# A perceiver layer with a mixture of experts: 64-row context tails, a routine for up to 96 left-over tokens of an expert, and a group split into halves

## The chip, the cores and the metric

The kernel runs on one core of a Trainium2 chip, in fp32. The metric is the device time of one execution, in microseconds. Three runs of the kernel before took 663.93, 663.94 and 664.02 us, so the median is 663.94 us.

## What is computed

There are 8 batches of 64 latent rows (x, width 512) and a context of 1601 rows of width 512 for each batch. Three residual blocks follow each other, each on a layer-normalized x:

```
x = x + relu( softmax( p (ctx W^T + b)^T ) ctx W^T + b )          p = layernorm(x)
x = x + attention block: causal linear attention (16 heads of 64, features elu(q proj) + 1),
        then a gelu MLP of width 2048, each on a layernorm with gain and shift
x = x + mixture of experts: 8 experts, each token sent to its best two, weights = softmax of the two logits,
        expert(x) = (silu(x w0) * (x w1)) wo        hidden width 1024
```

The first block's softmax runs over all 1601 context rows of a batch. The router picks two of eight experts for each of the 512 tokens, so there are 1024 pairs of token and expert, and how many fall to each expert is known only while the kernel runs.

## The kernel before

**Attention to the context.** The 512 latent rows stand in four tiles (NT = 4) of 128 rows; a tile holds two batches, 64 rows of each. `key_group(t, g)` multiplies the tile with a quarter of its two batches' transposed context (401 or 398 keys) into scores; when the fourth quarter is there, `softmax(t)` follows. `turn_scores(t)` transposes the exponentials back (three banks of 512 keys and one of what is left), and `weigh(t, g)` multiplies them with 512 context rows at a time, for both batches. 1601 rows are 3 x 512 and a tail of 65, which is loaded as a tile of 65 partitions, two batches beside each other (line 188), and multiplied at line 487. The result is scaled by 1 / sum on VectorE (line 495), transposed (`turn_av`) and multiplied with W (`attended`). The loop over t writes this order out by hand: between `weigh` steps of tile t stand the key groups of tiles t + 1 and t + 2, and for the last two tiles the value products (`values`, line 537) of the next block.

**The stream of loads.** Nearly all big inputs are loads of about 1 MB issued by SyncE (SP) in one list, `order`, built ahead of time; `issue_to` (lines 177 to 195) gives them out in that order as buffers of a ring of 12 come free. Each issue takes the next of eight semaphores and waits until the load that had it before has landed, so about eight loads are under way. For tile t the list has rows 0, keys 2 of the next tile, rows 1, keys 3, rows 2, the tail, then keys 0 and 1 of tile t + 2. Some small loads don't belong to the list: `late_loads` (lines 407 to 412: zeroes for a spare part of the output and for a table, b2 to all partitions, and the small projection twice) is issued when the loop reaches t = 1, after `weigh(1, 2)`, and so is `centre_router` (lines 544 to 557: eight TensorE instructions with 8 columns, and one on VectorE).

**The attention block and the MLP** run from about 172 to 405 us on TensorE without a gap that matters, and the change doesn't touch them.

**The experts.** For each expert e the first 128 of its tokens are one whole tile; the rows are gathered by an indirect DMA on GpSimd (`fetch`, line 1136) and transposed (`turn_tile`, line 1154). `whole_tile` multiplies them with four quarters of the up weights (line 1200; a quarter is 256 columns of w0 and 256 of w1), gates them on ScalarE and VectorE (lines 1163 and 1165), transposes the hidden values (line 1171) and accumulates the output (line 1208). `add_rows` scales the output by the gate on ScalarE (line 1180) and adds it to the result in memory by an indirect DMA (line 1181); these additions follow each other.

What an expert has beyond 128 tokens is found from `count` at run time. With 129 to 160 tokens `few` is 1 and `group(e)` runs right behind the whole tile: up to 32 rows, with the four quarters of the weights in four column groups of the array at once (line 1238), one gate, two transposes, line 1249 for the four partial outputs, and a product with `fold` (line 1259) that adds the four. With more than 160, all the rest goes to whole tiles of their own at the end of the program (`big_tile`, `all_big`), which load that expert's weights once more. The branches are at line 1429 (a group) and line 1433 (a big tile). All engines take them: each has read the counts into registers (`load_few`, `load_big`). An engine that skips a body waits for its own earlier work and raises its semaphores by what the body would have.

PSUM has two sets of banks here: `side_bank(0)` and `y_bank(0)` for whole tiles, `side_bank(1)` (two banks) and `y_bank(1)` (one) for groups, and one bank for transposed tokens.

Of the kernel before, what the change touches and what calls it, by code (L numbers as in the profile page):

```python
# [15 lines left out]
F32 = mybir.dt.float32  # L16
AF = mybir.ActivationFunctionType
ALU = mybir.AluOpType
# [9 lines left out]
TAIL = LK - NG * GK  # L28
# [7 lines left out]
R = P // NQ  # L36
NI = B * S // P
# [9 lines left out]
def perceiver_kernel(  # L47
# [127 lines left out]
    def issue_to(n):  # L175

        while issued[0] < min(n, len(order)):
# [8 lines left out]
            elif key[0] == "tail":  # L186
                t_ = tails.tile([P, 2, D], F32, tag="tail", name="_".join(str(k) for k in key))
                nc.sync.dma_start(t_[:TAIL, :, :], src)
# [261 lines left out]
    def turn_scores(t):  # L450
# [5 lines left out]
        for g in range(NG + 1):  # L456
# [6 lines left out]
            else:  # L463
                nc.tensor.transpose(bank[:TAIL, :P], scores[:, NG * GK : LK], ident)
                nc.scalar.copy(e_t[:TAIL, 4 * NG, :], bank[:TAIL, :P])

    all_av, all_xo = {}, {}

    def weigh(t, g):
# [15 lines left out]
        if g == NG - 1:  # L485
            for h in range(2):
                nc.tensor.matmul(
                    av[h * S : (h + 1) * S, :],
                    e_t[:TAIL, 4 * NG, h * S : (h + 1) * S],
                    need("tail", t)[:TAIL, h, :],  # L490
                    start=False,
                    stop=True,
                )
            av_sb = all_av[t] = xa2.tile([P, D], F32, tag="tmp", name=f"av_sb_{t}")
            nc.vector.tensor_scalar(av_sb, av, all_rinv[t], None, ALU.mult)
# [66 lines left out]
    for t in range(NT):  # L562
# [15 lines left out]
        if t == NT - 3:  # L578
            late_loads()
            centre_router()  # L580
# [530 lines left out]
    if True:  # L1111
# [36 lines left out]
        def turn_tile(key, n=P):  # L1148
# [8 lines left out]
            xg_t = moe2.tile([P, KC, n], F32, tag=f"xgT{n}", name=f"xgT_{key[0]}_{key[1]}")  # L1157
# [18 lines left out]
        def add_rows(key, y, n, side):  # L1176
# [3 lines left out]
            nc.scalar.activation(y_sb[:n, :], y[:n, :], AF.Copy, scale=gate[:n, :])  # L1180
# [10 lines left out]
        def whole_tile(key, up_of, down_of, between=lambda k: None):  # L1191
# [5 lines left out]
            def up(q):  # L1197
                bank = side_bank(0, f"up_{nm}_{q}")
# [4 lines left out]
                return gated(0, bank, f"{nm}_{q}")  # L1203
# [10 lines left out]
            h_t0 = hidden_t(0, hid0, f"{nm}_0")  # L1214
            hid2 = up(2)
            y = y_bank(0, f"y_{nm}")
            down(0, h_t0)
            h_t1 = hidden_t(0, hid1, f"{nm}_1")
            between(0)
            hid3 = up(3)  # L1220
            h_t2 = hidden_t(0, hid2, f"{nm}_2")
            down(1, h_t1)
            between(1)
            h_t3 = hidden_t(0, hid3, f"{nm}_3")
# [3 lines left out]
            add_rows(key, y, P, 0)  # L1228

        def group(e, up_of, down_of):  # L1230
# [4 lines left out]
            bank = side_bank(1, f"up_{nm}")  # L1235
            for c in range(KC):
                for q in range(NQ):
                    nc.tensor.matmul(  # L1238
                        bank[q * R : (q + 1) * R, :],
                        xg_t[c],  # L1240
                        up_of[q][:, c, :],
                        start=(c == 0),
                        stop=(c == KC - 1),
                    )
            h_t = hidden_t(1, gated(1, bank, nm), nm)
            bank = side_bank(1, f"yq_{nm}")
            for j in range(2):
                for q in range(NQ):
                    nc.tensor.matmul(
                        bank[q * R : (q + 1) * R, :],  # L1250
                        h_t[:, j, q * R : (q + 1) * R],
                        down_of[q // 2][:, 2 * (q % 2) + j, :],
# [3 lines left out]
            parts = moe2.tile([P, D], F32, tag="parts", bufs=1, name=f"parts_{nm}")  # L1256
            evacuate(parts, bank)
            y = y_bank(1, f"y_{nm}")
            nc.tensor.matmul(y[:R, :], fold, parts, start=True, stop=True)
            add_rows((e, 1), y, R, 1)  # L1260

        if True:
# [8 lines left out]

            few = moe.tile([P, NE], F32, name="few")
            more = moe.tile([P, NE, NI - 1], F32, name="more")
            nc.vector.tensor_scalar(more[:, :, 0], count, float(P + R), None, ALU.is_gt)
            nc.vector.scalar_tensor_tensor(few, count, float(P), more[:, :, 0], ALU.is_gt, ALU.subtract)
# [4 lines left out]
            def load_few():  # L1280
                _, values = nc.values_load_multi_w_load_instructions(
                    few_i, min_val=0, max_val=1, skip_runtime_bounds_check_because=counted
# [5 lines left out]
            control = moe.tile([1, 1 + 2 * NBIG], mybir.dt.int32, name="control")  # L1288
# [242 lines left out]
```

## Time and profile before

| what | value |
|---|---|
| median of three runs | 663.94 us |
| the profiled execution's own time | 665.04 us |
| its span, first to last instruction | 663.3 us |
| mean granted TensorE clock | 0.987 |
| TensorE waiting for context rows (line 477) | 6.3 us, 4 times |
| first up product of the experts starts | 417.26 us |
| groups that ran | experts 0, 3 and 5 |
| whole tiles at the end | 1 |
| last matmul ends | 651.98 us |
| e_up loads, 1 MB each | 32 and 4 for the whole tile at the end |

The profile is one execution. A row of a timeline has the start in us, the length, the engine, the line of the code, the operation with its output and inputs, the shape and a count; in brackets stands how long the engine had been idle and what ended that. TensorE does an fp32 product in two instructions, so "x32" is 16 products. A row of stretches has its bounds, its length, the busy time of PE (TensorE), PEld (its weight loads), DVE (VectorE), ACT (ScalarE) and POOL (GpSimd), each with its number of instructions, then the granted clock as a share of full speed, the busy share of the 16 DMA engines, and GB/s. A name with a q, such as POOLq, is that engine's sequencer. In the 40 slices of the page one slice is 16.6 us, and a digit is a share in tenths.

### The profile page before, as it was taken

The numbers are of one execution on the slowest core, as the hardware profiler recorded it, in microseconds if no ns is written. First come the engines' busy times: TensorE is split into PE (matmuls) and PEld (weight loads), VectorE is DVE, ScalarE is ACT, GpSimd is POOL, SyncE is SP. The second block draws the span as 40 slices with busy tenths as digits, with TensorE's granted clock in tenths as the row PEclk, the third lists the DMA queues.
The fourth block names the chain that finished last, engine by engine and source line by source line (L and its number), as shares of the span: only waits on it lengthen the run. The fifth ranks groups of instructions, "written<-read, shape, count | busy, mean of one in ns | idle before, by whom it ended". The sixth has DMA issues, their size and how long they took to land. (4 is left out here: it accounts for less than half of the span.)

```text
span 663.3 us, 6862 instructions
## 1 busy us (share of the span) xinstructions
PE 624.8 (94%) x2688; PEld 292.5 (44%) x2688; DVE 175.4 (26%) x421; ACT 128.9 (19%) x242; POOL 61.8 (9%) x82
## 2 busy tenths in 40 slices
PE   4998999899999999999999999999999899999993
PEld 3743434243444444455444458434444344344441
DVE  4011323123315878760000045311211011100100
ACT  2241222220132222031101211211111111111110
POOL 2000000000000000050000012240201202200000
PEclk9998999899999999999999999999999999999997
DMA  8999999999430303030311313139379567594611
GB/s 325 418 424 398 423 393 422 381 394 417 178 126 3 126 1 127 1 126 1 126 64 63 116 74 133 64 96 365 139 280 377 178 279 246 202 385 155 263 16 19
DMA packets 24224, 138.08 MB, mean 208 GB/s; under 512 B 4164, under 2 KB 4164, under 8 KB 11896
## 3 DMA queue, kind: packets, MB, share of 16 engines
q1 hardware_dynamic: 20056, 129.90, 49.8%
q0 software_dynamic: 3024, 6.58, 4.4%
q10 hardware_dynamic: 1104, 1.07, 0.5%
q8 instruction: 25, 0.41, 0.3%
q14 instruction: 15, 0.12, 0.0%
HBM read 132.56 MB, written 4.97 MB: 207 GB/s over the span
## 5 line engine op out<-in xcount | busy, mean ns | idle before, releaser
L1200 PE MATMUL up<-e_up,xgT 128*128 128x512 f32 x224 | 100.2, 595 | 1.2 <-PEq L1429 1.2
L1200 PEld LDWEIGHTS up<-e_up,xgT 128*128 128x128 f32 x224 | 40.9, 190 | 50.4 <-issue 50.4
L1208 PE MATMUL y<-e_wo,hidT 128*128 128x512 f32 x128 | 61.0, 599 | 0.0
L477 PE MATMUL av<-ctx,eT 128*64 128x512 f32 x192 | 51.3, 648 | 6.3 <-DMA ctx<-in_ctx_dram 6.3
L1165 DVE TENSOR_TENSOR mid<-up,act 128x256 f32<-128x256 f32 x35 | 14.8, 425 | 159.4 <-ACT act L1163 159.4
L809 PE MATMUL hid<-v_sb,w 128*128 128x512 f32 (+2 forms) x144 | 56.6, 545 | 0.0
L830 PE MATMUL mlp<-w,hid_sb 128*128 128x512 f32 x112 | 51.0, 597 | 0.0
L428 PE MATMUL sc<-ctxT,pw_t 128*64 128x401 f32 (+1 forms) x256 | 46.6, 501 | 0.0
L809 PEld LDWEIGHTS hid<-v_sb,w 128*128 128x128 f32 x144 | 26.2, 190 | 29.1 <-issue 27.3
L1163 ACT ACTIVATE act<-up 128x256 f32<-128x256 f32 x35 | 13.3, 384 | 103.7 <-PE up L1200 94.9
L1181 POOL DMA_INDIRECT out_dram<-y_sb,dst_late x11 | 16.8, 1530 | 159.9 <-ACTq L1429 103.7
L824 POOL TENSOR_TENSOR xin<-xin,b_bc 128x512 f32<-128x512 f32 x4 | 5.1, 1265 | 283.2 <-DVE rstd_h L766 279.0
L830 PEld LDWEIGHTS mlp<-w,hid_sb 128*128 128x128 f32 x112 | 20.7, 190 | 23.5 <-issue 23.4
L1208 PEld LDWEIGHTS y<-e_wo,hidT 128*128 128x128 f32 x128 | 22.4, 190 | 19.5 <-issue 19.1
L428 PEld LDWEIGHTS sc<-ctxT,pw_t 128*64 128x64 f32 x256 | 20.6, 136 | 23.4 <-issue 21.7
L477 PEld LDWEIGHTS av<-ctx,eT 128*64 128x64 f32 x192 | 14.7, 146 | 36.1 <-issue 27.5
L728 PE MATMUL wo<-wo,a_t 128*128 128x512 f32 x64 | 29.1, 600 | 0.6 <-DVE a_t L704 0.6
L617 PE MATMUL wk<-h_t,wk 128*128 128x512 f32 x64 | 29.5, 603 | 0.0
L617 PE MATMUL wq<-h_t,wq 128*128 128x512 f32 x64 | 29.4, 602 | 0.0
L537 PE MATMUL v<-wv,h_t 128*128 128x512 f32 x64 | 28.7, 597 | 0.6 <-DVE h_t L524 0.6
L702 DVE RECIPROCAL rden<-rden 128x512 f32<-128x512 f32 x8 | 26.8, 3353 | 0.3
L878 DVE TENSOR_TENSOR xs<-mlp,xs 128x512 f32<-128x512 f32 x3 | 2.1, 692 | 86.6 <-PE mlp L830 86.6
(245 smaller groups left out, 642.6 us busy)
## 6 DMA issues: line engine op xcount, KB each, us to landing
e_up<-in_L_ffn_up_dram SPq DMA_DIRECT2D x32, 1024.0 KB, 7.7
ctx<-in_ctx_dram SPq DMA_DIRECT2D x24, 1024.0 KB, 17.1
ctxT<-in_ctx_T_dram SPq DMA_DIRECT2D x24, 802.0 KB, 15.7
e_wo<-in_L_ffn_wo_dram SPq DMA_DIRECT2D x16, 1024.0 KB, 10.6
w<-in_L_attn_w_dram SPq DMA_DIRECT2D x8, 1024.0 KB, 9.8
ctxT<-in_ctx_T_dram SPq DMA_DIRECT2D x8, 796.0 KB, 16.4
big_up<-in_L_ffn_up_dram SPq DMA_DIRECT2D x4, 1024.0 KB, 7.7
wv<-in_L_attn_wv_dram SPq DMA_DIRECT2D x2, 1024.0 KB, 13.0
```

The lines of the kernel that those rows point to most:

```text
L428: nc.tensor.matmul(sc[h * S : (h + 1) * S, :width], pw_t[:, c, (2 * t + h) * S : (2 * t + h + 1) * S], keys[h][:, c, :], start=(c == 0), s ...
L477: nc.tensor.matmul(av[h * S : (h + 1) * S, :], e_t[:, 4 * g + j, h * S : (h + 1) * S], rows[h][:, j, :], start=(g == 0 and j == 0), stop=F ...
L537: nc.tensor.matmul(bank, h_t[:, c, t * P : (t + 1) * P], wv_n[:, c, :], start=(c == 0), stop=(c == KC - 1))
L617: nc.tensor.matmul(bank, w[:, c, (j % 4) * P : (j % 4 + 1) * P], h_t[:, c, :], start=(c == 0), stop=(c == KC - 1),)
L702: nc.vector.reciprocal(rden, rden)
L728: nc.tensor.matmul(wo_banks[t], a_t[:, j, t * P : (t + 1) * P], wo_r[j // 4][:, j % 4, :], start=(j == 0), stop=(j == nj - 1),)
L809: nc.tensor.matmul(hid_banks[f][:, tokens], w[:, c, (f % 4) * P : (f % 4 + 1) * P], h2_t[:, c, tokens], start=(c == 0), stop=(c == KC - 1),)
L830: nc.tensor.matmul(acc[t], hid[:, t * P : (t + 1) * P], need("w2", f // 4)[:, f % 4, :], start=(f == 0), stop=(f == FF // P - 1),)
L1165: nc.vector.tensor_tensor(hid, bank[:, FQ:], act, ALU.mult)
L1181: nc.gpsimd.indirect_dma_start(out=out, out_offset=bass.IndirectOffsetOnAxis(ap=dst[:n, :], axis=0), in_=y_sb[:n, :], in_offset=None, boun ...
L1200: nc.tensor.matmul(bank, xg_t[c], up_of[q][:, c, :], start=(c == 0), stop=(c == KC - 1))
L1208: nc.tensor.matmul(y, h_t[:, j, :], w[:, 2 * (q % 2) + j, :], start=(q + j == 0), stop=(q + j == NQ))
```

## The change

- **Level tails.** TAIL is 64; the tail tile holds all 128 partitions, 64 rows of one batch above 64 of the other, and beside them the last context row of each batch, repeated on its 64 partitions. Two products of 64 x 64 take the place of the transpose of 65 keys, the tail's products take 64 rows each, and the last row is added on VectorE by a multiply-add, after which the scaling by 1 / sum is an operation of its own.
- **Late loads and the router's centring** run at t = 2 in place of t = 1.
- **Three groups.** `few` is 2 for 129 to 160 tokens, 1 for 161 to 224 (REST = 96 left over) and 0 otherwise; only more than 224 goes to whole tiles. `three_groups` does up to 96 rows in three groups of 32, their steps interleaved. Gathers of left-over tokens take 96 rows for 32, and the scaling of the three groups' output is on VectorE.
- **The group** is split: each half of its hidden width has its own gate, and the first half is transposed between the second half's products. Outputs are made in halves of 256 columns.
- **Branches.** Both kinds of groups stand in one outer branch. What experts 6 and 7 have beyond 128 tokens and the big tiles stand in one branch ahead of expert 7's whole tile; `any` is set when any of it is there. Big tiles use group banks and expert 6's weight buffers. Instructions with a hint about a later branch are put into the whole tile's first `between`.
- Smaller: expert 7's left-over tokens are transposed during expert 6; three more small VectorE operations find `few`, three more find `any`, and one more register is loaded on each engine.

The core of the diff:

```diff
-TAIL = LK - NG * GK
+TAIL = LK - NG * GK - 1
...
+REST = 3 * R
...
-                nc.sync.dma_start(t_[:TAIL, :, :], src)
+                nc.sync.dma_start(t_, src)
...
-                nc.tensor.transpose(bank[:TAIL, :P], scores[:, NG * GK : LK], ident)
-                nc.scalar.copy(e_t[:TAIL, 4 * NG, :], bank[:TAIL, :P])
+                for h in range(2):
+                    part = slice(h * S, (h + 1) * S)
+                    nc.tensor.matmul(
+                        bank[part, :S],
+                        scores[part, NG * GK : NG * GK + TAIL],
+                        ident[part, part],
+                        start=True,
+                        stop=True,
+                    )
+                nc.scalar.copy(e_t[:, 4 * NG, :S], bank[:, :S])
...
-                    e_t[:TAIL, 4 * NG, h * S : (h + 1) * S],
-                    need("tail", t)[:TAIL, h, :],
+                    e_t[h * S : (h + 1) * S, 4 * NG, :S],
+                    need("tail", t)[h * S : (h + 1) * S, 0, :],
...
             av_sb = all_av[t] = xa2.tile([P, D], F32, tag="tmp", name=f"av_sb_{t}")
-            nc.vector.tensor_scalar(av_sb, av, all_rinv[t], None, ALU.mult)
+            nc.vector.scalar_tensor_tensor(
+                av_sb, need("tail", t)[:, 1, :], all_scores[t][:, LK - 1 : LK], av, ALU.mult, ALU.add
+            )
+            nc.vector.tensor_scalar(av_sb, av_sb, all_rinv[t], None, ALU.mult)
...
         weigh(t, 2)
-        if t == NT - 3:
+        if t == NT - 2:
...
         def group(e, up_of, down_of):
...
+            split = "p (w n) -> p w n"
+            halves = [slice(h * P, (h + 1) * P) for h in range(2)]
+            hid, h_t = [], {}
+
+            def turn(j):
+                bank = side_bank(1, f"ht_{nm}_1") if j else y_bank(1, f"ht_{nm}_0")
+                nc.tensor.transpose(bank[:, :P], hid[j], ident)
+                h_t[j] = moe2.tile([P, P], F32, tag="hidT1", name=f"hidT_{nm}_{j}")
+                (nc.scalar.copy if j else nc.vector.tensor_copy)(h_t[j], bank[:, :P])
+
+            for h in range(2):
+                bank = side_bank(1, f"up_{nm}_{h}")
+                for c in range(KC):
+
+                    if h == 1 and c == KC - 1:
+                        turn(0)
+                    for q in range(NQ):
+                        nc.tensor.matmul(
+                            bank[q * R : (q + 1) * R, : 2 * P].rearrange(split, w=2),
+                            xg_t[c],
+                            up_of[q][:, c, :].rearrange(split, w=2)[:, :, halves[h]],
+                            start=(c == 0),
+                            stop=(c == KC - 1),
+                        )
+                act = moe2.tile([P, P], F32, tag="act1", name=f"act_{nm}_{h}")
+                nc.scalar.activation(act, bank[:, :P], AF.Silu)
+                hid.append(moe2.tile([P, P], F32, tag="mid1", name=f"mid_{nm}_{h}"))
+                nc.vector.tensor_tensor(hid[h], bank[:, P : 2 * P], act, ALU.mult)
+            sums = {}
+
+            def down(j, n):
+                if j == 0:
+                    sums[n] = y_bank(1, f"yq_{nm}_1") if n else side_bank(1, f"yq_{nm}_0")
...
+                        sums[n][q * R : (q + 1) * R, : D // 2],
+                        h_t[j][:, q * R : (q + 1) * R],
+                        down_of[q // 2][:, 2 * (q % 2) + j, n * D // 2 : (n + 1) * D // 2],
                         start=(j == 0),
                         stop=(j == 1),
                     )
...
+            down(0, 0)
+            turn(1)
+            down(0, 1)
+            parts = []
+            for n in range(2):
+                down(1, n)
+                parts.append(moe2.tile([P, D // 2], F32, tag="parts", name=f"parts_{nm}_{n}"))
+                (nc.scalar.copy if n else nc.vector.tensor_copy)(parts[n], sums[n][:, : D // 2])
+            y = side_bank(1, f"y_{nm}")
+            for n in range(2):
+                nc.tensor.matmul(
+                    y[:R, n * D // 2 : (n + 1) * D // 2], fold, parts[n], start=True, stop=True
+                )
             add_rows((e, 1), y, R, 1)
+
+        def three_groups(e, up_of, down_of):
+
+            nm = f"{e}_1"
+            xg = fetched[e, 1]
...
+            hid, h_t, sums, parts = {}, {}, {}, {}
+
+            def up(g):
+                bank = side_bank(1, f"up_{nm}_{g}")
+                for c in range(KC):
+                    tokens = turned[e, 1][c] if g == 0 else xg_t3[:, c, g * R : (g + 1) * R]
+                    for q in range(NQ):
+                        nc.tensor.matmul(
+                            bank[q * R : (q + 1) * R, :],
+                            tokens,
+                            up_of[q][:, c, :],
+                            start=(c == 0),
+                            stop=(c == KC - 1),
+                        )
+                hid[g] = gated(1, bank, f"{nm}_{g}")
+
+            def turn(g):
+                bank = y_bank(1, f"ht_{nm}_{g}")
+                for j in range(2):
+                    nc.tensor.transpose(bank[:, j * P : (j + 1) * P], hid[g][:, j * P : (j + 1) * P], ident)
+                h_t[g] = moe2.tile([P, 2, P], F32, tag="hidT3", name=f"hidT_{nm}_{g}")
+                nc.vector.tensor_copy(h_t[g].rearrange("p j q -> p (j q)"), bank[:, : 2 * P])
+
+            def down(g):
+                bank = side_bank(1, f"yq_{nm}_{g}")
+                for j in range(2):
+                    for q in range(NQ):
+                        nc.tensor.matmul(
+                            bank[q * R : (q + 1) * R, :],
+                            h_t[g][:, j, q * R : (q + 1) * R],
+                            down_of[q // 2][:, 2 * (q % 2) + j, :],
+                            start=(j == 0),
+                            stop=(j == 1),
+                        )
+                parts[g] = moe2.tile([P, D], F32, tag="parts3", name=f"parts_{nm}_{g}")
+                if g < 2:
+                    nc.scalar.copy(parts[g], bank)
+                else:
+                    nc.vector.tensor_copy(parts[g][:, : D // 2], bank[:, : D // 2])
+                    nc.scalar.copy(parts[g][:, D // 2 :], bank[:, D // 2 :])
+
+            def folded(g):
+                for n in range(2):
+                    cols = slice(n * D // 2, (n + 1) * D // 2)
+                    nc.tensor.matmul(
+                        y[g * R : (g + 1) * R, cols], fold, parts[g][:, cols], start=True, stop=True
+                    )
+
+            up(0)
+            up(1)
+            turn(0)
+            up(2)
+            turn(1)
+            down(0)
+            down(1)
+            turn(2)
+            y = side_bank(1, f"y3_{nm}")
+            folded(0)
+            down(2)
+            folded(1)
+            folded(2)
+            add_rows((e, 1), y, REST, 1, by_vector=True)
...
-            nc.vector.tensor_scalar(more[:, :, 0], count, float(P + R), None, ALU.is_gt)
-            nc.vector.scalar_tensor_tensor(few, count, float(P), more[:, :, 0], ALU.is_gt, ALU.subtract)
+            nc.vector.tensor_scalar(more[:, :, 0], count, float(P + REST), None, ALU.is_gt)
+            nc.vector.tensor_scalar(few, count, float(P), 2.0, ALU.is_gt, ALU.mult)
+            over = moe.tile([P, NE], F32, name="over_few")
+            nc.vector.tensor_scalar(over, count, float(P + R), None, ALU.is_gt)
+            nc.vector.tensor_tensor(few, few, over, ALU.subtract)
+            nc.vector.tensor_tensor(few, few, more[:, :, 0], ALU.subtract)
...
+            def few_tokens(e, up_of, down_of):
+                with tc.If(few_of[e] > 0, label=f"few_{e}"):
+                    with tc.If(few_of[e] == 1, label=f"three_{e}"):
+                        three_groups(e, up_of, down_of)
+                    with tc.If(few_of[e] == 2):
+                        group(e, up_of, down_of)
+
+            def hint_ahead(e):
+
+                labels = ["last_branches"] if e == NE - 2 else [f"few_{e}", f"three_{e}"]
+                with tc.block():
+                    for label in labels:
+                        tc.mark_branch_hint_location(label, "LikelyTaken", engines=every)
...
-                    if k == 2:
+                    if k == 2 and e < NE - 1:
                         turn_tile((e, 1), R)
+                    if k == 2 and e == NE - 2:
+                        turn_tile((NE - 1, 1), R)
...
                 down_of = [need("e_wo", e, n) for n in range(2)]
+                if e == NE - 1:
+
+                    with tc.If(listed["any"] > 0, label="last_branches"):
+                        few_tokens(e - 1, *last_weights)
+                        few_tokens(e, up_of, down_of)
+                        all_big(0)
+                if e == NE - 2:
+                    last_weights.extend((up_of, down_of))
                 whole_tile((e, 0), up_of, down_of, between)
...
-                        fetch((e + 2, i), R if i else P)
+                        fetch((e + 2, i), REST if i else P)
...
-                with tc.If(few_of[e] > 0):
-                    group(e, up_of, down_of)
-
-            def all_big(j):
-                with tc.If(listed["big"] > j):
-                    big_tile(j)
-                    if j + 1 < NBIG:
-                        all_big(j + 1)
-
-            all_big(0)
```

In `weigh` the tail's products and in `issue_to` the tail's load follow from the new layout, which the host prepares. In `three_groups` the hidden values go through `gated`, as before.

## The prediction

> **What bounds the kernel now.** I read the page first, then TensorE's timeline around the attention and the experts, then the stretches of 2 us, then the records of the branches and of the end.
>
> ```profile
> PE 624.8 (94%) x2688; PEld 292.5 (44%) x2688; DVE 175.4 (26%) x421; ACT 128.9 (19%) x242; POOL 61.8 (9%) x82
> PEclk9998999899999999999999999999999999999997
> GB/s 325 418 424 398 423 393 422 381 394 417 178 126 3 126 1 127 1 126 1 126 64 63 116 74 133 64 96 365 139 280 377 178 279 246 202 385 155 263 16 19
> ```
>
> TensorE is the bound by its share, but two things differ by stage: in the first ten slices the DMA moves about 420 GB/s without a pause, and PEclk dips twice. The attention to the context is where both meet (TensorE's timeline):
>
> ```profile
> 60.99 4.91 PE L477 MATMUL av<-ctx,eT 128*64 128x512 f32 x13 [2.14 <-DMA ctx<-in_ctx_dram]
> ...
> 93.36 3.22 PE L477 MATMUL av<-ctx,eT 128*64 128x512 f32 x13 [1.00 <-DMA ctx<-in_ctx_dram]
> ...
> 127.73 6.16 PE L477 MATMUL av<-ctx,eT 128*64 128x512 f32 x13 [2.66 <-DMA ctx<-in_ctx_dram]
> ...
> 135.11 3.70 PE L537 MATMUL v<-wv,h_t 128*128 128x512 f32 x8
> ```
>
> The same 13 matmuls take 3.22 us after a wait of 1.00 us, but 4.91 and 6.16 after waits of 2.14 and 2.66. After 135 us nothing waits for the context any more. The stretches say why:
>
> ```profile
> 122.00:124.00 2.00, 1.51 (x10) 0.43 (x7) 0.00 (x0) 0.41 (x1) 0.00 (x0) 1.00 1.01 422
> 124.00:126.00 2.00, 1.04 (x2) 0.19 (x2) 1.79 (x1) 1.46 (x2) 0.00 (x0) 1.00 1.09 254
> 126.00:128.00 2.00, 0.27 (x2) 0.27 (x4) 0.03 (x1) 1.72 (x2) 0.00 (x0) 0.71 0.97 287
> 128.00:130.00 2.00, 2.00 (x6) 0.50 (x6) 0.00 (x0) 0.00 (x0) 0.00 (x0) 0.50 1.01 408
> ```
>
> The last columns are clock, DMA share and GB/s: busy engines, but only 254 and 287 GB/s. The same dip stands at 58-62 (275, 381), 90-94 (266, 354) and 146-150 us (254, 274), each where the 4 KB packets of a "tail" load of 65 rows are under way. Then the clock is half.
>
> The experts, at one group (TensorE's timeline):
>
> ```profile
> 441.05 3.64 PE L1238 MATMUL up<-e_up,xgT 128*32 128x512 f32 x32
> 445.68 0.44 PE L1171 MATMUL ht<-ident,mid 128*128 128x128 f32 x2 [0.99 <-DVE mid L1165]
> 446.73 1.92 PE L1249 MATMUL yq<-e_wo,hidT 128*32 128x512 f32 x16 [0.61 <-DVE hidT L304]
> 449.35 1.04 PE L1259 MATMUL y<-parts,fold 128*32 128x512 f32 x2 [0.70 <-ACT parts L306]
> 450.32 7.13 PE L1200 MATMUL up<-e_up,xgT 128*128 128x512 f32 x16
> ```
>
> A group costs 450.32 - 441.05 = 9.27 us, 2.3 of it stalls; three run (experts 0, 3, 5). The whole tile at the end:
>
> ```profile
> 628.90 0.65 PE L1154 MATMUL xgt_big<-ident,xg_big 128*128 128x128 f32 x4 [0.32 <-PEq L1429]
> ...
> 648.38 3.60 PE L1208 MATMUL y_big<-big_wo,hidT_big 128*128 128x512 f32 x8
> ```
>
> From 628.58 (its predecessor's end) to 651.98 it holds TensorE for 23.4 us. The inputs, put through the reference, give 133, 104, 217, 159, 87, 132, 70, 122 tokens per expert: the three groups fit, and the whole tile is expert 2's other 89.
>
> **A. Level tails, late loads (attention).** A tail DMA grows from 65 to 128 rows of 4 KB, by 0.258 MB, 0.6 us at 420 GB/s. Against it goes its dip: for the second, (420-266+420-354) x 2 us = 0.44 MB, 1.0 us; for the third (166+133) x 2 = 0.60 MB, 1.4 us; for the first (145+39) x 2, 0.9 us. The rows here that don't divide by 16 are the only ones with a dip; the Trainium skill (DMA: Bandwidth & Descriptors, "Why a DMA increments its semaphore by 16 and not by 1") has the number of DMA engines as the largest divisor up to 16, 13 for 65 rows and 16 for 128. I take the dip as gone; if it stays, nothing is gained by it. The late loads (0.58 MB, 1.4 us) stood on SP's queue at 104.9 to 113.6 us, just ahead of the context rows waited for at 127.73. They move behind the last rows, the fourth tail, wv, wq and wk. Behind them then waits wo, first used at 261 us, 100 us of cover; b2, proj and the zeroes are used later than 180 us.
>
> The rows waited for land earlier by 0.3 (first tail: 0.9-0.6), 0.4 (second), 1.4 (third, behind them) and 1.4 (late loads): 3.5 us, at 124.2. Counting 2.5 us per 1 MB load and 2.0 per key load on from the first dip, each wait in between is then 1.0 us or less, so the clock holds: 13 matmuls at 3.22 for 6.16, and the tail's at full speed, 2.9 us. The Trainium skill (TensorE: Matmul & The Clock Gate, "What's actually happening") has the clock fall after an idle window of about 3.4 us; by that rule neither wait would have cost anything and only 3.5 us would come. The rows show the fall after 2.14, so I take 2.9 more. The router's centring (L548, 8 instructions, 1.06 us) ran at 97.8 inside time that the next wait swallowed; at t = 2 it is on the path: +1.06. The tail's scores cost two matmul pairs for one transpose (0.27 us row), +0.1 to 0.2 a tile, free but for the last. VectorE's extra op (0.75 us, row of av_sb) fits: av_sb was ready 1.9 us before turn_av began. Sum -3.5 - 2.9 + 1.1 + 0.2 = **-5.1**. At best -6.9 (landing at 123.2, which the count from the first dip gives, and the tail's matmuls closer). If the dip and the half clock stay, late loads -1.4 against two longer tails +1.2 and +1.1 leave +0.9.
>
> **B. Three groups for expert 2's tile.** Up: 3 x 3.6 (L1238); hidden transposes 3 x 0.22; down 3 x 1.8 (L1249); four transposes of 96 rows 0.43; fold, twelve passes of 256 columns at 0.22 = 2.6, of which 0.5 runs beside another column group. 19.5; the order interleaves the groups, so act + mid (0.99) and copies (0.6-0.7) lie behind a 3.6 or 1.8 us block. With 0.5 for what is left: 20.0. Against 23.4: **-3.4** (19.2 to 21).
>
> **C. The split group.** Half an up is 32 instructions of 256 columns: 1.8. Two halves 3.6; its first transpose (0.11) lies within the second half. ACT and DVE on half the columns: 0.27 and 0.29 (128x128 rows), so 0.76 for 0.99. Then down(0,0) 0.43 after 0.2; wait 0.14 for the second hidden half; transpose 0.11; 0.43; wait 0.15; 0.43, 0.43; wait 0.17; two folds 0.86: 3.35 after the up. 7.1 with the transpose; I take 7.3, saving 2.0 x 3 = **-6.0** (1.5 to 2.4 each).
>
> **D. Branches.** Every skipped body makes TensorE wait for itself: 0.30 ("up <- PEq L1429", four, 1.2 us in the waits; the fifth is in the 23.4). After: experts 1, 4 and the last block 0.3 each; 0, 3, 5 skip the three groups and 2 skips the group, each with one more compare directly behind (0.19): 0.5. 2.9 - 1.2 = **+1.7**. A skip on POOL holds its queue for INC_SWDGE_SEM (0.7-1.0 us); behind it stand gathers used 20 us later. Gathers of 96 rows for 32 add 0.05 us each; expert 0's landed 2.2 us before use. Three more small DVE ops at 421.5 (0.17 each) and in list_big stand before DVE waits of 3 us. The third register load (0.3 us) hides in PE's lead.
>
> Whether the jump's target is there, no hint being in this trace, is bounded by these records (count, least/median/most ns, first and last start):
>
> ```profile
> L1429 PEldq COMPARE_BRANCH  x11: 70/188/339, 438.1 to 625.1; - x11
> L1433 PEldq COMPARE_BRANCH  x3: 70/188/3638, 628.8 to 652.9; - x3
> L1433 POOLq INC_SWDGE_SEM  x1: 1005/1005/1005, 657.8 to 657.8; - x1
> L1527 POOLq DRAIN  x3: 46/109/3500, 659.0 to 663.1; - x3
> ```
>
> Skipping one group costs 0.34 at most, skipping six whole tiles 3.64. The Trainium skill (Runtime: NRT & Kernel Launch, "Instruction fetch mechanics") says a taken branch past the prefetched window stalls for a fetch: it speaks against the longer bodies. PE's sequencer reaches a branch some 3.4 us early (625.1 against 628.58), so even 3.64 shows as 0.2. I take nothing more; 12 x 3.64 at the far end, below nothing impossible.
>
> **E. The end.** Before, TensorE's end at 651.98 is followed by ACT, scatter (653.0), landing (657.6), then by the skip's INC 1.0, DRAIN 3.5 and 0.8: 11.3 us. After, no branch stands behind the last tile: the INC goes, and DRAIN can start behind the scatter's 1.55 and end at about 658.1, beside the landing and SP's 0.8 of waits. Saved 4.3; if DRAIN waits for the landing, 1.4. I take **-3.7**, nearer the first, since DRAIN began with nothing outstanding.
>
> Sum: -5.1 - 3.4 - 6.0 + 1.7 - 3.7 = -16.5 on the profiled 665.04 (span 663.3 + 1.7): 648.5. The median, 663.94, is 1.1 under the profiled run: **647.4**.
>
> **Rivals.** (1) Dip and half clock stay: A is +0.9, 6.0 worse: 653.4. For it: the rule alone explains the dip. 0.15. (2) Slower: fetches. If hints that say "taken" spoil the fall-through (few_0, few_2, three_2, few_3, few_5) and the seven jumps find nothing ahead, and the lead is spent, each costs 3.64 on TensorE: 43.7, 691. It turns slower from 16.5 / 12 = 1.4 us each. Against it: the lead, and 0.34 at most for L1429. 0.07. (3) Some of these are exposed, 4 us in all: 651.4. 0.13. (4) The counts on the chip send expert 2 to the whole tile still: B is lost, and its weights now load into expert 6's buffers, only after that expert (7.7 us to landing): 659. 0.02. (5) Shorter still, A at -6.9 and C at 2.4: 644.4. 0.10. The likeliest has 0.53.
>
> The range 642.5 to 654 leaves out (2), and the outer ends of (1) and (3). A measurement tells 0.2% (1.3 us): faster 0.92, same 0.01, slower 0.07.
>
> **What would show it.** PEclk without the dips at 60 and 128; 420 GB/s while a tail lands; values (L537) starting at 130 for 135.1; three_groups 20 us, a group 7.3; branches under 0.4 us; the end 7.6 us behind TensorE's last matmul. Wrong would be a half clock at another wait, a PE branch of microseconds behind a hint, stalls of 0.5 within the split group.

## The result, and the profile after

Five runs of the kernel after have a median of 653.12 us (652.2 to 653.31), five of the kernel before beside them 663.94 (661.87 to 664.82). The ratio is 0.984, 95% interval 0.982 to 0.986. The forecast of 647.4 had the sign and, with 642.5 to 654.0, the range; it was 5.7 us too low. A later set of runs on another chip gave the same code 659.27 us; that is told with the last experiments. In the profiled run (652.34 us, span 650.2, clock 0.995) the page shows TensorE's busy time, the granted clock and GB/s:

```profile
PE 622.0 (96%) x2956; PEld 293.3 (45%) x2956; DVE 180.8 (28%) x438; ACT 128.6 (20%) x246; POOL 62.1 (10%) x82
PEclk9999999999999999999999999999999999999998
GB/s 325 417 423 422 424 425 422 427 426 423 219 98 34 98 1 131 1 130 0 129 64 67 81 98 106 108 94 349 123 368 46 199 204 306 185 367 191 282 18 16
```

Both dips of PEclk are gone, and slices 2 to 10 move 417 to 427 GB/s. TensorE's timeline at the context rows, and where the value products begin:

```profile
60.20 3.65 PE L487 MATMUL av<-ctx,eT 128*64 128x512 f32 x14 [0.50 <-DMA ctx<-in_ctx_dram]
91.69 3.65 PE L487 MATMUL av<-ctx,eT 128*64 128x512 f32 x14 [0.28 <-DMA ctx<-in_ctx_dram]
123.14 3.65 PE L487 MATMUL av<-ctx,eT 128*64 128x512 f32 x14 [0.25 <-DMA ctx<-in_ctx_dram]
128.64 1.53 PE L551 MATMUL v<-wv,h_t 128*128 128x512 f32 x3
```

The waits sum to 1.0 us where they were 6.3, no matmul behind them is slow, and the values start at 128.64 for 135.11. Two stretches of 2 us around the third wait, whose last columns are clock, DMA share and GB/s:

```profile
124.00:126.00 2.00, 2.00 (x11) 0.71 (x8) 0.55 (x1) 1.41 (x2) 0.00 (x0) 1.00 1.05 442
126.00:128.00 2.00, 2.00 (x9) 0.47 (x7) 0.16 (x1) 0.31 (x2) 0.00 (x0) 1.00 0.98 414
```

They stood at 254 and 287 GB/s. The group of expert 0 (TensorE's timeline):

```profile
436.19 3.23 PE L1278 MATMUL up<-e_up,xgT 128*32 128x256 f32 x56 [1.26 <-ACTq L1551]
439.35 0.33 PE L1267 MATMUL ht<-ident,mid 128*128 128x128 f32 x1
439.61 0.64 PE L1278 MATMUL up<-e_up,xgT 128*32 128x256 f32 x8
440.15 0.64 PE L1295 MATMUL yq<-e_wo,hidT 128*32 128x256 f32 x8
441.05 0.33 PE L1267 MATMUL ht<-ident,mid 128*128 128x128 f32 x1 [0.25 <-DVE mid L1288]
441.30 1.50 PE L1295 MATMUL yq<-e_wo,hidT 128*32 128x256 f32 x24
442.92 1.05 PE L1313 MATMUL y<-parts,fold 128*32 128x256 f32 x4
443.90 0.70 PE L1224 MATMUL up<-e_up,xgT 128*128 128x512 f32 x1
```

443.90 - 436.19 = 7.71 us for 9.27, but 1.26 us of waiting stands ahead of it, released by ScalarE's sequencer at the branch. The records of the branches and of the end (count, least/median/most ns, first and last start):

```profile
L1550 PEldq COMPARE_BRANCH  x6: 87/100/3317, 431.9 to 584.7; - x6
L1551 PEldq COMPARE_BRANCH  x5: 84/327/388, 432.1 to 584.9; - x5
L1553 PEldq COMPARE_BRANCH  x8: 73/192/402, 435.1 to 596.1; - x8
L1703 POOLq DRAIN  x3: 46/120/6823, 642.5 to 649.9; - x3
```

The two skips of an expert's whole branch (experts 1 and 4) took 3.32 and 3.31 us in spite of their hints. DRAIN starts beside the last scatter and ends at 649.3, 1.7 behind the landing at about 647.6; the last matmul ends at 641.76 and the span 8.4 us later, for 11.3.

The ledger of the two profiled runs: the experts' first up starts at 411.07 for 417.26 (-6.2); from there to the last matmul 230.69 us for 234.72 (-4.0); the end -2.9. Together -13.1 us of span.

### The profile page after: what moved, and what is told of

Read it like the earlier page. It is cut to its first block, busy times and chain, and to the rows that moved or that the text cites. A ratio compares the mean times of both kernels' runs of the same rounds, so it can differ in the third digit from the quotient of the medians.

```text
span 650.2 us, 7530 instructions
## 1 busy us (share of the span) xinstructions
PE 622.0 (96%) x2956; PEld 293.3 (45%) x2956; DVE 180.8 (28%) x438; ACT 128.6 (20%) x246; POOL 62.1 (10%) x82
## 3 DMA queue, kind: packets, MB, share of 16 engines
q10 hardware_dynamic: 1104, 1.07, 0.5%
## 4 chain that ended last, share of the span: by engine, by line
PE 47%; DMA 25%; issue 22%; DVE 2%; POOL 1%; POOLq 1%; ACT 0%; SPq 0%; DVEq 0%; ACTq 0%
DMA out_dram<-y_sb,dst_late 11%; DMA ctx<-in_ctx_dram 10%; PE hid L823 8%; PE mlp L844 7%; PE wk L631 4%; PE wq L631 4%; PE v L551 4%; PE wo L742 4%; PE pw L374 3%; DMA ctxT<-in_ctx_T_dram 2%; PE av L487 2%; PE sc L429 2%; PE pr_wq L647 1%; PE xo L521 1%; PE qk L673 1%
## 5 line engine op out<-in xcount | busy, mean ns | idle before, releaser
L487 PE MATMUL av<-ctx,eT 128*64 128x512 f32 x192 | 46.6, 597 | 1.0 <-DMA ctx<-in_ctx_dram 1.0
L1205 POOL DMA_INDIRECT out_dram<-y_sb,dst_late x12 | 18.3, 1524 | 177.7 <-ACT y_sb L1204 79.1
## 6 DMA issues: line engine op xcount, KB each, us to landing
e_wo<-in_L_ffn_wo_dram SPq DMA_DIRECT2D x16, 1024.0 KB, 11.2
```

The source lines that it names most:

```text
L487: nc.tensor.matmul(av[h * S : (h + 1) * S, :], e_t[:, 4 * g + j, h * S : (h + 1) * S], rows[h][:, j, :], start=(g == 0 and j == 0), stop=F ...
L1205: nc.gpsimd.indirect_dma_start(out=out, out_offset=bass.IndirectOffsetOnAxis(ap=dst[:n, :], axis=0), in_=y_sb[:n, :], in_offset=None, boun ...
```

## The experiments

Each set of runs also timed the kernel before on its own chip, and the ratios are to that; between two sets the same code moved by 6 us (part 4). Waits of TensorE are in order of time.

**1. The parts of the attention, each alone.** Five kernels, all from the kernel before.

Tails only (the new tail layout in the load, in `turn_scores` and in `weigh`, nothing else):

> The kernel before with the 64-row tails alone; late loads and the router's centring stay at t = 1, experts untouched. If the dips of the 65-row loads are what held the attention back, the rows waited for at 127.7 us land 2.1 us sooner (0.3 + 0.4 + 1.4) and no wait is long enough to halve the clock (2.9 us): values (L551) start at 130, the whole at 5 us under before. If the late loads carried the gain, the wait ahead of weigh(2, 2) stays over 2 us, the clock still halves there, and no more than 1 us is gained.

659.84 us, ratio 0.995 (0.994 to 0.997). Waits for the context 1.15, 0.56, 0.34 and 1.30, no half clock, 410 to 442 GB/s where the dips were, values at 129.52. That is 3.7 us under the kernel before beside it (663.51), where 5 were expected.

Late loads only:

```diff
-        if t == NT - 3:
+        if t == NT - 2:
             late_loads()
             centre_router()
```

> The kernel before with late loads and the router's centring at t = 2 alone; tails of 65 rows. With the dips as the cause: the rows of t = 2 land 1.4 us sooner, the centring costs 1.06 on the path, the dips at 58, 90 and 124 us stay and the clock halves at 61 at least: between -0.5 and 0 us. With the late loads as the cause: the wait and the half clock at 128 us are gone and 3 us or more are gained.

661.44 us, ratio 0.998 (0.997 to 0.999): 2.1 us less, between the two expectations (0.5 at most, 3 at least). The dips stay, as these stretches of its trace show (last column), but each wait is under 2 us and no clock falls:

```profile
90.00:92.00 2.00, 2.00 (x10) 0.53 (x6) 0.15 (x1) 0.77 (x2) 0.00 (x0) 1.00 1.11 273
92.00:94.00 2.00, 0.53 (x4) 0.24 (x6) 1.67 (x1) 1.41 (x2) 0.00 (x0) 1.00 0.90 318
```

Two of its waits in TensorE's timeline, both with the 13 matmuls at full speed:

```profile
93.47 3.22 PE L477 MATMUL av<-ctx,eT 128*64 128x512 f32 x13 [1.48 <-DMA ctx<-in_ctx_dram]
...
126.14 3.22 PE L477 MATMUL av<-ctx,eT 128*64 128x512 f32 x13 [1.69 <-DMA ctx<-in_ctx_dram]
```

Both:

> Both of these, experts as before: the whole of part A. The trace after has the first value product 6.5 us and the experts' first product 6.2 us sooner, so 6.2 us under before (657.7 for 663.9), if the part is independent of the experts. If the two edits only work together this is more than the sum of the two alone; if either is enough, it equals that one.

659.25 us, ratio 0.994 (0.992 to 0.996); values at 128.76, experts' first up at 411.20. By the trace that is all of the change's gain ahead of the experts, to 0.1 us. Against the median of the kernel before, 663.51, it is 4.3 us and not the 6.2 expected: the 6.2 are counted from a profiled run of the kernel before that was itself 1.1 us over its median. The parts don't add (3.7 and 2.1 alone, 4.3 together): either alone lets the clock hold.

What makes the dip? A tail load of 80 rows, which is 16 equal shares:

```diff
-                nc.sync.dma_start(t_[:TAIL, :, :], src)
+                nc.sync.dma_start(t_[:80, :, :], src)
```

> The kernel before, its tail tile loaded with 80 rows (15 rows of zeroes behind the 65, which nothing reads); all products as before. 80 divides into 16 equal shares, 65 only into 13. If the number of DMA engines or uneven shares make the dip, it is gone at 0.06 MB more: GB/s stays above 400 at 58, 90, 124 and 146 us and 4 to 5 us are gained. If the dip is there because only little more than half the partitions are written, it stays as it was and the time is within 0.5 us of before.

664.95 us, ratio 1.003 (1.001 to 1.004). The dips stay, and so does a half clock. Its stretches around the third wait (clock, DMA share and GB/s last):

```profile
124.00:126.00 2.00, 1.08 (x4) 0.19 (x2) 1.27 (x1) 1.88 (x2) 0.00 (x0) 1.00 1.11 344
126.00:128.00 2.00, 0.00 (x0) 0.00 (x0) 0.56 (x1) 1.41 (x2) 0.00 (x0) 1.00 0.95 252
128.00:130.00 2.00, 1.21 (x6) 0.58 (x8) 0.00 (x0) 0.31 (x2) 0.00 (x0) 0.91 1.01 309
```

Two waits in its timeline, the clock full behind the first and half behind the second:

```profile
93.88 3.22 PE L477 MATMUL av<-ctx,eT 128*64 128x512 f32 x13 [1.89 <-DMA ctx<-in_ctx_dram]
128.79 4.92 PE L477 MATMUL av<-ctx,eT 128*64 128x512 f32 x13 [2.92 <-DMA ctx<-in_ctx_dram]
```

So it is not the 13 shares of 65 rows that make the dip. Left were two readings: the load writes only a part of the partitions, or its shares are not those of a 128-row load. A load of 112 rows tells them apart, the same edit with 112:

> The kernel before with a tail load of 112 rows in place of 65 (the added 47 rows are zeroes that nothing reads), so 16 equal shares of 7 rows. The 80-row load, 16 equal shares of 5, kept the dip, so equal shares are not what counts. Theory 'where the rows land': the dip comes from a load that writes only a part of the partitions; 112 of 128 partitions are nearly all, so the dips are mostly gone, no stretch of 2 us under 350 GB/s around 60, 92 and 126 us, and no wait for context above 2.1 us, about 661 to 662. Rival 'shares that don't follow the partition blocks': any row count other than 128 gives dips as deep as with 80 rows (250 to 320 GB/s) and a half clock at one of the waits, 664 to 666.

666.36 us, ratio 1.003 (1.002 to 1.005). Waits of 2.48, 2.17 and 2.94 us, a half clock behind each. Two stretches of the third dip:

```profile
126.00:128.00 2.00, 1.31 (x6) 0.27 (x2) 0.84 (x1) 1.45 (x2) 0.00 (x0) 1.00 1.04 240
128.00:130.00 2.00, 0.00 (x0) 0.00 (x0) 0.98 (x1) 1.41 (x2) 0.00 (x0) 0.95 1.00 256
```

Writing nearly all partitions doesn't help: the first reading falls. In these runs only 128 rows are free of the dip; 65, 80 and 112 have it. The DMA engines are as busy in the dips as outside (share 0.90 to 1.11), so the same work takes them longer; why was not settled.

What halves the clock is not the length of a wait by itself. Within a trace the changes of the clock stand whole multiples of 3.41 us apart: in the kernel before, half clocks begin at 62.00 and 126.85, 19 x 3.413 us from each other. Here are stretches of 3.41 us, cut at those places; the second number is TensorE's busy time, and the clock stands before the last two. First the kernel before, then the 80-row load around its wait of 1.89 us:

```profile
58.59:62.00 3.41, 1.27 (x7) 0.45 (x8) 1.82 (x1) 1.52 (x2) 0.00 (x0) 1.00 1.00 320
62.00:65.41 3.41, 3.41 (x12) 0.98 (x10) 0.00 (x0) 0.40 (x2) 0.00 (x0) 0.50 0.99 406
```

```profile
92.10:95.51 3.41, 1.63 (x8) 0.63 (x10) 1.56 (x1) 2.73 (x3) 0.00 (x0) 1.00 0.97 287
95.51:98.92 3.41, 3.41 (x18) 1.31 (x14) 0.49 (x1) 0.00 (x0) 0.00 (x0) 1.00 1.02 418
```

In all fourteen traces, from the first full clock to the last matmul, the clock is half behind every such stretch with TensorE busy for 1.27 us or less, and behind none with 1.6 or more. So the idle time within one stretch counts: 2.14 us of it were enough, 1.8 were not, and several short waits can add up to it. Part 4 has such a case. It is read from these traces; no experiment tests it by itself.

**2. The split group alone**, put into the kernel before in place of its group, under the old branches:

> The kernel before with the split group alone (same branch, 65-row tails, whole tile at the end). In the trace after a group takes 7.71 us for 9.27. If that saving is the group's own, 3 x 1.55 = 4.6 us come off: a ratio of 0.993. If the group was only worth it with the new branches and banks, or loses again what it gains, less than 2 us. My forecast had 7.3 us a group, 6.0 us in all.

658.73 us, ratio 0.992 (0.989 to 0.994). From the experts' first up to the last matmul 229.9 us for 234.7, so -4.8 or 1.6 a group. No wait stands ahead of a group there, so the 1.26 us of the kernel after come from its branches. With no wait ahead of it, expert 0's group there takes 7.66 us (439.49 to 447.15).

**3. The wait ahead of a group.** TensorE's first weight load of a group waits for ScalarE's semaphore. ScalarE raises it when it has skipped the three groups, and that skip stands behind its scaling of the whole tile's output (0.69 us). First, the order of the branches:

```diff
-                    with tc.If(few_of[e] == 1, label=f"three_{e}"):
-                        three_groups(e, up_of, down_of)
                     with tc.If(few_of[e] == 2):
                         group(e, up_of, down_of)
+                    with tc.If(few_of[e] == 1, label=f"three_{e}"):
+                        three_groups(e, up_of, down_of)
```

> The kernel after with the order of the two inner branches swapped: the group stands ahead of the three groups. In the trace after, the gap ahead of a group is 0.8 to 1.3 us and ends when ScalarE has skipped the three groups. If the group's first weight load waits for ScalarE because the skipped body ahead of it used the same banks, the gap ahead of the groups of experts 0, 3 and 5 falls to 0.5 us or less, and 0.3 to 0.8 us come back behind each: between -1.5 and 0 us against the kernel after (653). If the gap is just the price of a skipped branch with many instructions, it only moves: 653 as before, with the gap behind the group.

650.36 us (650.22 to 650.65), ratio 0.979 (0.977 to 0.982); on another chip, 2.8 us under the kernel after, more than the 1.5 expected, though the profiled spans differ by 1.3 only. Expert 3's group now starts without a wait, and half a microsecond stands behind it instead:

```profile
533.49 3.23 PE L1278 MATMUL up<-e_up,xgT 128*32 128x256 f32 x56
...
540.15 1.05 PE L1313 MATMUL y<-parts,fold 128*32 128x256 f32 x4
541.75 1.10 PE L1224 MATMUL up<-e_up,xgT 128*128 128x512 f32 x2 [0.55 <-PEq L1553]
```

The waits at all branches sum to 3.63 us for 5.36. Second, the order of work: the scaling and adding of a whole tile moved behind its branch (experts 0 to 6):

```diff
-            add_rows(key, y, P, side)
+            pending.append((key, y, P, side))
...
                 if e < NE - 2:
                     few_tokens(e, up_of, down_of)
+                while pending:
+                    add_rows(*pending.pop())
```

> The kernel after with the whole tile's scaling and its addition to the output moved behind the branch of its expert (experts 0 to 5). If TensorE's gaps are there because ScalarE comes to its skip only behind the 0.69 us scaling of the whole tile, ScalarE has skipped before TensorE arrives: gaps of 0.5 at experts 0, 3, 5 and 0.3 at expert 1 for 1.26, 1.14, 0.82 and 0.78, 2.4 us less than after (650.7). If TensorE's own sequencer makes them (instruction fetch), they stay and the time is 653.

650.96 us, ratio 0.982 (0.979 to 0.985). The waits ahead of the three groups' 1.26, 1.14 and 0.82 became 0.44, 0.43 and 0.43: ScalarE's place in line is shown as the cause. In all 3.93 us. The wait behind expert 1 was expected to fall to 0.3 and rose from 0.78 to 0.98: TensorE's own jump over that branch took 3.52 us here, the one behind expert 4 3.75.

Third, the hints left out:

> The kernel after without any hint ahead of the branches (the hints inside the big tiles' branch stay; it isn't taken). If the jumps find their target anyway, or TensorE's sequencer is early enough, no branch shows more than about 0.4 us of idle time and the time is that of after within 0.5 us. If the hints carry it, each of seven jumps costs up to 3.64 us less a lead of about 3 us, 0.6 us or more: 4 us or more over after, with idle time of TensorE behind compare-and-branch instructions of microseconds, most of all at expert 7, where 2000 instructions are skipped.

651.9 us, ratio 0.982 (0.979 to 0.984), no slower than with them. The jump over expert 5's three groups took 3.88 us for 0.33 and the one ahead of the last tile 3.44 for 0.35, but nearly all of it lies in the sequencer's lead; the waits sum to 5.66 us.

**4. The end, the best order, and the kernel after once more.** These, and the 112 rows, ran on one chip. The last branch moved behind expert 7's whole tile:

> The kernel after with its last branch (what experts 6 and 7 have beyond 128 tokens, and the big tiles; not taken with this input) moved behind expert 7's whole tile. Theory: the end was shortened because no skip stands behind the last tile. Then POOL's semaphore increment (about 1 us) and its DRAIN of 3.5 us come behind the last landing again, the span ends 11.3 us behind TensorE's last matmul in place of 8.4, and TensorE saves the 0.3 us wait ahead of the last tile: about 2.6 us longer than the kernel after, 655 to 656. Rival: the end is set by the landing and a fixed close, and the shorter end of the kernel after comes from elsewhere: 8.4 us again, so 652 to 653.

659.91 us, ratio 0.994 (0.991 to 0.996). From the last matmul (646.36) to the end of the span (657.6) it takes 11.2 us, and the records of its end are like those of the kernel before:

```profile
L1598 POOLq INC_SWDGE_SEM  x1: 1014/1014/1014, 652.2 to 652.2; - x1
L1703 POOLq DRAIN  x3: 46/114/3494, 653.3 to 657.3; - x3
```

So the place of the skip makes the difference of 3 us at the end. Expert 5's group holds the clock's other case. It has waits of 1.25 and 1.07 us, each shorter than the 1.89 that left the clock full, and they fall into one stretch of 3.41 us:

```profile
594.13:597.54 3.41, 1.19 (x16) 0.25 (x16) 0.54 (x2) 0.28 (x1) 1.98 (x2) 1.00 0.80 195
597.54:600.95 3.41, 3.31 (x26) 1.44 (x27) 0.47 (x2) 0.31 (x2) 0.00 (x0) 0.50 0.81 298
```

The total, 4 us over what was expected, is not to be read from the branch's place, because of the next:

> The kernel after, unchanged, on the same chip as its three variants: 652 to 653.3, span 650 to 651.5, so that what the variants gain is compared with it on one chip.

659.27 us (655.6 to 660.88), ratio 0.991 (0.988 to 0.993), with the kernel before at 664.11 beside it. The same code took 6 us more than in its first five runs, and the expectation failed. Its attention is the same (first up at 411.11, end 8.2 us); the 7 us stand between 510 and 602. TensorE's timeline behind expert 2's three groups:

```profile
508.23 2.03 PE L1374 MATMUL y<-parts,fold 128*32 128x256 f32 x8
513.35 8.80 PE L1224 MATMUL up<-e_up,xgT 128*128 128x512 f32 x16 [3.09 <-issue]
```

The record of the branch that stands there:

```profile
L1553 PEldq COMPARE_BRANCH  x8: 73/188/2729, 435.2 to 603.4; - x8
```

The stretches behind it, with the clock in the column before the last two:

```profile
513.00:515.00 2.00, 1.66 (x3) 0.71 (x4) 0.00 (x0) 0.00 (x0) 0.00 (x0) 0.66 1.05 332
515.00:517.00 2.00, 2.00 (x4) 0.93 (x3) 0.00 (x0) 0.00 (x0) 0.00 (x0) 0.50 0.86 245
```

A branch that took at most 0.40 us in the first profiled run took 2.73. It is the last of expert 2's branch, behind the skip of the group, and that skip waits for TensorE's own work: there is no lead left, and all of it shows. The 3.09 us of idleness then halve the clock, so 16 matmuls take 8.80 for 7.11.

The long branch is a wait for instructions. The trace lists loads of instructions as a DMA queue of their own, q8, in pieces of 16 KB. One starts within the slow branch (510.45 to 513.18); in the first profiled run one came 3 us ahead of the branch (507.2 to 508.3), and none falls within it. The queue in these two windows (packets, MB, share of the 16 engines), the slow one first:

```profile
q8 instruction: 1, 0.02, 2.5%
```

```profile
q8 instruction: 1, 0.02, 5.2%
```

In the fourteen traces, each of the 22 branches of TensorE that took over 2.7 us has such a load starting in it, none of those up to 0.64 us has, and there is one between, of 2.16 us, whose load had just begun. Why the load came late is open. The rest is in the groups of experts 3 and 5 (expert 5's rows):

```profile
597.59 0.64 PE L1278 MATMUL up<-e_up,xgT 128*32 128x256 f32 x8
599.45 0.64 PE L1295 MATMUL yq<-e_wo,hidT 128*32 128x256 f32 x8 [1.23 <-issue]
601.16 0.33 PE L1267 MATMUL ht<-ident,mid 128*128 128x128 f32 x1 [1.07 <-DVE mid L1288]
```

There the two waits were 0 and 0.25. The profile names "issue" for the first, that is nothing it shows. The kernel with the branch moved has the group waits too (0.93; 1.25 and 1.07) on that chip, but not the slow branch. No load in q8 falls on these waits of expert 5's group, so their cause stays open, and so does why all this came in these runs and not in the first.

Last, the swap and the late scaling together:

> The kernel after with the group's branch ahead of the three groups', and with the whole tile's scaling moved behind its branch. The swap alone gave 650.4 with waits of 3.6 us in all at the branches, the late scaling alone 651.0 with 3.9. Theory: the two take away the same wait ahead of a group (ScalarE's skip of the three groups behind its scaling), so together they give hardly more than the better one: the wait of 0.8 ahead of expert 2's three groups falls to about 0.4, 650.0. Rival: they add up, 1.7 and 1.4 us off the waits of 5.4 of the kernel after, 649.2 or less.

649.8 us (649.38 to 650.12), ratio 0.978 (0.977 to 0.979): on the same chip 9.5 us below the kernel after, but some 7 of them are the slow branch and the group waits, which this kernel does not show there. Against the swap alone its gain is 0.6 us, inside the intervals, and its waits at branches sum to 3.42 us for 3.63; the two take away the same wait. It is the shortest of all these kernels, and its five runs lie within 0.8 us.

## Why the prediction was right or wrong, step by step

**A, -5.1: -6.2 at the experts' first up, -6.5 at the values, 4.3 between medians.** In the trace landing and clock came as reckoned, and a little more; part of that is the profiled run it is counted from. But the reason given for the dip was wrong, and that 128 rows are free of it was luck as far as that reason goes: the prediction drew it from the rule of the Trainium skill (DMA: Bandwidth & Descriptors, "Why a DMA increments its semaphore by 16 and not by 1") that 65 rows go to 13 engines. With 80 and 112 rows the same rule gives 16, and the stretches still fall to 252 and 240 GB/s. The rule may well hold; it doesn't explain the dip, and rival (1), that the dip stays, was weighed by a rule that doesn't bear on it. That the clock falls after waits shorter than the 3.4 us that the Trainium skill gives for an idle window (TensorE: Matmul & The Clock Gate, "What's actually happening") was right. The traces show stretches of that length, but not that one has to be idle all through: 2.14 us of idleness in it were enough. That a wait's length alone decides, as the prediction read it, was too simple, and did no harm here because its waits fell to 0.5 us and less.

**B, three groups in 20.0: 20.05.** Right (490.07 to 510.12; its parts make 19.4 and not 19.5).

**C, 7.3 a group: 7.71,** so -4.7 for -6.0. The mechanism is right, the size was off: from the first product to the end of the second half 3.96 us where 3.7 was reckoned with the transpose, and 3.75 behind it for 3.35. Each transpose holds TensorE for 0.25 us where 0.11 was put, which is nearly half of the excess, and the wait for `mid` is 0.25 where 0.14 was put.

**D, branches +1.7: +4.2.** This step failed. Waits at branches were 5.36 us for 1.2 before, ahead of the groups of experts 0, 3 and 5 1.26, 1.14 and 0.82 where 0.5 was put. The prediction said "0, 3, 5 skip the three groups and 2 skips the group, each with one more compare directly behind (0.19): 0.5", and followed TensorE's own skip alone. A group's first weight load waits also for ScalarE's skip, and ScalarE comes to it late. Expert 1's 0.78 ends with ScalarE's skip as well, but TensorE's own jump of 3.32 us sticks out of the lead and ends only 0.3 us before. The prediction's "even 3.64 shows as 0.2" counted one lead for every branch; expert 2's last compare stands behind a wait for TensorE itself and has none. In the first runs that cost nothing more, in the last ones 3.09 us and a half clock. Rival (3), some fetches exposed, is what came in the last runs, in which the long branch holds a load of instructions; rival (2), with twelve of them, did not come.

**E, -3.7: -2.9.** The skip behind the last tile goes, as reckoned, and DRAIN starts early, but it ends 1.7 us behind the landing and not beside it, between the two bounds of 4.3 and 1.4. Moving the branch back puts the 11.2 us back.

The steps' sum misses by 3.4 us of the span: +2.5 from D, +1.3 from C, +0.8 from E, -1.1 from A, and a remainder of -0.1. The other 2.3 us are in how a profiled run stands to the median: 1.1 above it before (at a clock of 0.987; that kernel's runs at 0.993 or more took 661.5 to 662.5), 0.8 below it after, and 0.4 more around the span.

## What to carry to other kernels

A branch costs what the slowest engine that the next work waits for needs to get past it, so look at what each of them still has in line ahead of the skip, and put the body that runs most often first. A jump of 3 to 4 us is free only while the sequencer is ahead of its engine; behind a skip that waits for the engine itself nothing hides it, and such a place can cost nothing in one set of runs and microseconds in the next. Where idle time stands close to the amount at which the clock halves, small things each remove the whole penalty, and their gains don't add.

## What the runs showed of the hardware that was not expected

- Tail loads of 65, 80 and 112 rows of 4 KB took the stream from about 420 GB/s to 240 to 320 while they were under way; the load of 128 rows, the largest of them, did not.
- TensorE's clock changed only at places whole multiples of 3.41 us apart. It was half behind each such stretch in which TensorE was idle for 2.14 us or more, in one wait or several, and behind none with 1.8 or less.
- Branches took TensorE's sequencer 2.7 to 3.9 us where a load of instructions starts in them, with hints and without, and 0.64 or less where none does.
- DRAIN on GpSimd took 3.5 us from its start when it began behind the last landing, and ended 1.7 us behind the landing when it began ahead of it.
